# A four-layer graph network on one core: layer 0's input is transposed by DMA in 16-bit halves, and attention's scores and products become separate steps

## Chip, core and metric

The kernel runs on one core of a Trainium2 chip. The metric is device time in microseconds (us) of one execution. The kernel before takes 2674.66 us (median of 3 runs, 2673.68 to 2675.3). The engines are PE (TensorE, matrix products), DVE (VectorE), ACT (ScalarE), POOL (GpSimd) and SP (SyncE, whose queue issues nearly all DMAs here).

## What is computed

The input is x, 64 graphs of 256 nodes with 256 features (f32), and adj, 64 matrices of 256 x 256 (int32). Four layers follow each other; each one is `x = layernorm(x + layer(x, adj))`. Cut to what matters here:

```python
# layer 0: masked attention, 4 heads of 64
q, k, v = x @ Wq.T + bq, x @ Wk.T + bk, x @ Wv.T + bv
attn = softmax(where(adj == 0, NEG, q @ k.T * 64 ** -0.5))
x = layernorm(x + affine_layernorm(attn @ v @ Wo.T + bo))
# layer 1: masked attention on the normed x, 8 heads of 32, then an MLP of width 1024
n = affine_layernorm(x); a = x + softmax(mask(n @ n.T * 32 ** -0.5)) @ n
x = layernorm(x + a + gelu(affine_layernorm(a) @ W1 + b1) @ W2 + b2)
# layer 2: graph attention, one head; layer 3: an edge score by kind of edge, softmax, product
```

The first matmuls of layer 0 contract over the features of x. TensorE contracts over the partitions, so x must be brought with its features on the partitions ("features first"). In memory it lies with the nodes first.

## The kernel before

Two graphs make a group, so there are 32 groups. A group is a Python generator that yields after each step. The program interleaves the groups: in each period it goes through the digits of ORDER, and a digit d runs the next step of the group that started d periods ago. So about six groups are at work at any time. The written order is a wish: a scheduler then places each engine's instructions, only PE's own order is fixed as written.

```python
ORDER = "011225334342343542234235432323132121321132121"
io  = tile_pool(name="io", bufs=2)      # x0 and adj: two buffers each
act = tile_pool(name="act", bufs=3)     # xT, qT, kT, v, y, z, mask ...
ps_s = tile_pool(name="ps_s", bufs=2, space=PSUM)   # scores, two banks each
ps_m = tile_pool(name="ps_m", bufs=4, space=PSUM)   # everything else

def transposed(src, ...):               # PE transposes, then ACT copies out of PSUM
    for c in range(NC):                 # NC = 2 halves of the 256 features
        pt = to_psum(src, c, gs)        # 4 PE transposes of 128 x 128 f32 (L519)
        nc.scalar.copy(dst[:, c, on], pt[:, on])                     # L572
        # or, with scale and bias: nc.scalar.activation(...)         # L574

def attention(qT, kT, v, mask, hd, gamma, behind, tally=None):
    for i in range(G):                  # G = 2 graphs
        for cs in ((0, 1),) if m == 2 else ((0,), (1,)):
            es = scores(i, cs, ...)     # PE scores, ACT exp (L593), DVE mask (L595, L601)
            if before:
                products(*before)       # PE products of the scores of the step before
            go_on()                     # what stands behind a finished graph
            ...
            yield

def layer0(g, x, mask):
    xT = transposed(x)                  # 8 PE transposes a group, 2 ACT copies
    yield
    # WqT, WkT: 8 matmuls of 128 x 512, ACT adds the bias; yield after each; then WvT
    nc.gpsimd.tensor_tensor(x, x, over_blocks(beta0), ALU.add)       # L705
    # attention; behind it: oT * rr (L718), WoT (PE), y (L725), two norms
    # (statistics on DVE, rstd = (var + eps) ** -0.5 on GpSimd, L535 to L539), z (L547)

def layer1(xb, z, mask):
    zT = transposed(z, gamma1, beta1)   # PE transposes of z, ACT L574
    # attention with heads of 32, W1 with Gelu (L774); later W2 (hT), layers 2 and 3

def group(g):
    x, adj = (first, second)[g] if g < 2 else load_group(g)          # L439, L441
    yield
    adjb = io.tile([P, TB, N], BF16, name="adjb", bufs=1)
    nc.scalar.activation(adjb, adj, AF.Copy, accum_out=...)          # L875
    nc.scalar.activation(adj.bitcast(F32), adj, AF.Square, ...)      # L876
    yield
    pt = io.tile([P, G, QB, N], BF16, name="adjT", bufs=1)
    for t in range(TB):                 # 4 DMA transposes, two blocks of 128 x 128 each
        nc.sync.dma_start_transpose(pt[:, i, :, q * P:(q + 1) * P], adjb[:, t, :])   # L883
    yield
    mask = act.tile([P, G, QB * N], BF16, name="mask")
    nc.vector.scalar_tensor_tensor(mask, pt, 1.0, adjb, ALU.mult, ALU.min, ...)      # L886
    xb, z = yield from layer0(g, x, mask)
    ...
```

(Cut and shortened where "..." stands.) At the start the SP queue issues x and adj of group 0, then the weights and constants, then group 1 and the two large weights, and after those the first DMA transposes.

Of the kernel before, what the change touches and what calls it, by code (L numbers as in the profile page):

```python
# [8 lines left out]
F32 = mybir.dt.float32  # L9
BF16 = mybir.dt.bfloat16  # L10
I32 = mybir.dt.int32
U8 = mybir.dt.uint8
AF = mybir.ActivationFunctionType
ALU = mybir.AluOpType
AX = mybir.AxisListType

P = 128
N = 256
D = 256
NC = D // P  # L20
G = 2
QB = N // P
TB = G * QB
T = G * N
# [9 lines left out]
AT_ONCE = 3  # L34


ORDER = "011225334342343542234235432323132121321132121"
PREPARE = 5


# [355 lines left out]
def usual_input(ctx: ExitStack, tc: tile.TileContext, a: dict, out: bass.AP, flag: bass.AP):  # L396
# [7 lines left out]
    nc = tc.nc  # L404
    B = a["x"].shape[0]

    const = ctx.enter_context(tc.tile_pool(name="const", bufs=1))
    io = ctx.enter_context(tc.tile_pool(name="io", bufs=2))
    act = ctx.enter_context(tc.tile_pool(name="act", bufs=AT_ONCE))
# [24 lines left out]
    r_3 = const.tile([P, B // G, TB], F32, name="r_3")  # L434
    last = const.tile([P, B // G, TB], F32, name="last")

    def load_group(g):
        x0 = io.tile([P, TB, D], F32, name="x0")
        nc.sync.dma_start(x0, a["x"][g * G:(g + 1) * G].rearrange("b (q p) d -> p (b q) d", p=P))  # L439
        adj = io.tile([P, TB, N], I32, name="adj")  # L440
        nc.sync.dma_start(adj, a["adj"][g * G:(g + 1) * G].rearrange("b (q p) k -> p (b q) k", p=P))  # L441
        return x0, adj

    def load_rows(name, cols, queue=nc.sync):

# [17 lines left out]
        return t  # L463


    first = load_group(0)
    wqT = load_rows("L0_gnn_WqT", D, nc.scalar)
    wkT = load_rows("L0_gnn_WkT", D, nc.scalar)
    bq = load_column(a["L0_gnn_bq"], D, "bq", nc.scalar)
# [18 lines left out]
    beta2 = load_column(a["L1_gnn_beta2"], D, "beta2")  # L488
    b1 = load_column(a["L1_gnn_b1"], DFF, "b1")
    a0 = load_column(a["L3_gnn_a0"], D, "a0")  # L490
    second = load_group(1)
    w1 = load_rows("L1_gnn_W1", DFF)
    w2 = load_rows("L1_gnn_W2", D)

# [70 lines left out]
    def transposed(src, scale=None, bias=None, gs=ALL):  # L565

        on = tokens(gs)
        dst = act.tile([P, NC, T], F32, name="xT")
        for c in range(NC):
            pt = to_psum(src, c, gs)  # L570
            if scale is None:
                nc.scalar.copy(dst[:, c, on], pt[:, on])  # L572
            else:
                nc.scalar.activation(dst[:, c, on], pt[:, on], AF.Identity, bias=bias[:, c:c + 1], scale=scale[:, c:c + 1])  # L574
        return dst
# [56 lines left out]
    def attention(qT, kT, v, mask, hd, gamma, behind, tally=None):  # L632

        scale = hd ** -0.5
        m = P // hd
        before = sums = None
        after = []

        def go_on():
            for r in list(after):
                if next(r, END) == END:
                    after.remove(r)

        for i in range(G):
            for cs in ((0, 1),) if m == 2 else ((0,), (1,)):
                if cs[0] == 0 and gamma is not None:
                    sums = small.tile([P, QB, NC, 4], F32, name="r1")
                es = scores(i, cs, qT, kT, mask[:, i, :], hd, scale, sums)  # L650
                if before:
                    products(*before)
                go_on()
                if cs[0] == 0:
                    oT = att.tile([P, NC, N], F32, name="oT")
                    zs = att.tile([P, N], F32, name="zs") if sums is None else sums
                if before and before[1][-1] == NC - 1:
                    after.append(behind(before[0], before[5], before[6]))
                before = (i, cs, v, es, hd, oT, zs, gamma, tally)
                yield  # L660
        products(*before)
        after.append(behind(G - 1, oT, zs))
        yield
        while after:
            go_on()
            yield
# [19 lines left out]
            else:  # L686
                nc.vector.tensor_tensor(o, pm, extra[:, i * QB:(i + 1) * QB, 0:D], ALU.add)

    def layer0(g, x, mask):
        xT = transposed(x)  # L690
        yield
        qT = act.tile([P, NC, T], F32, name="qT")
        kT = act.tile([P, NC, T], F32, name="kT")
        for w, bcol, dst in ((wqT, bq, qT), (wkT, bk, kT)):
            for f in range(NC):
                pm = ps_m.tile([P, T], F32, name="pm")
                for c in range(NC):
                    matmul(pm, w[:, c, f * P:(f + 1) * P], xT[:, c, :], start=c == 0, stop=c == NC - 1)
                nc.scalar.activation(dst[:, f, :], pm, AF.Identity, bias=bcol[:, f:f + 1])
            yield  # L700
        v = act.tile([P, TB, D], F32, name="v")
        yield from project(v, xT, wvT, None)
        yield

        nc.gpsimd.tensor_tensor(x, x, over_blocks(beta0), ALU.add)  # L705
        y = act.tile([P, TB, D], F32, name="y")
        z = act.tile([P, TB, D], F32, name="z")
        xb = act.tile([P, TB, D], F32, name="xb", tag="v")

        def behind(i, oT, rz):  # L710

            rr = att.tile([P, NC, N], F32, name="rr")
            lines = dram.tile([NC, 2, N], F32, name="lines")
            nc.sync.dma_start(lines.rearrange("c h n -> (c h) n"), rz[0:P:32, :])
            for h in range(2):
                nc.sync.dma_start(rr[h * 64:h * 64 + 64, :, :], lines[:, h, :].unsqueeze(0).to_broadcast([64, NC, N]))
            yield
            nc.vector.tensor_tensor(oT, oT, rr, ALU.mult)  # L718
            yield
            pm = ps_m.tile([P, QB, D], F32, name="pm")  # L720
            for q in range(QB):
                for c in range(NC):
                    matmul(pm[:, q, :], oT[:, c, q * P:(q + 1) * P], woT[:, c, :],
                           start=c == 0, stop=c == NC - 1)
            nc.vector.tensor_tensor(y[:, i * QB:(i + 1) * QB, :], pm, over_blocks(bop, QB), ALU.add)  # L725
            yield
            mv, rstd = stats(y, i)
            for q, t in enumerate(blocks(i)):
                nc.vector.scalar_tensor_tensor(y[:, t, :], y[:, t, :], mv[:, q, 0:1], gamma0, ALU.subtract, ALU.mult)  # L729
                nc.vector.scalar_tensor_tensor(y[:, t, :], y[:, t, :], rstd[:, 0, q:q + 1], x[:, t, :],  # L730
                                               ALU.mult, ALU.add)
            yield
            mv, rstd = stats(y, i, twice=True)
            scaled(z, y, i, mv, rstd[:, 1])
            for q, t in enumerate(blocks(i)):
                nc.vector.scalar_tensor_tensor(xb[:, t, :], z[:, t, :], rstd[:, 0, q:q + 1], beta1r, ALU.mult, ALU.add)  # L736
            yield

        yield from attention(qT, kT, v, mask, 64, None, behind, [r_0[:, g * G + i:g * G + i + 1] for i in range(G)])
        return xb, z  # L740

# [127 lines left out]
        return (yield from values_of(lambda i, kc, q: e[:, i, at[kc][q]:at[kc][q] + P], x, D, x, r_3[:, g], gs, last[:, g]))  # L869

    def group(g):
        x, adj = (first, second)[g] if g < 2 else load_group(g)
        yield
        adjb = io.tile([P, TB, N], BF16, name="adjb", bufs=1)
        nc.scalar.activation(adjb, adj, AF.Copy, accum_out=there[:, g:g + 1])  # L875
        nc.scalar.activation(adj.bitcast(F32), adj, AF.Square, bias=minus_half, accum_out=edges[:, g:g + 1])  # L876
        yield


        pt = io.tile([P, G, QB, N], BF16, name="adjT", bufs=1)  # L880
        for t in range(TB):
            i, q = divmod(t, QB)
            nc.sync.dma_start_transpose(pt[:, i, :, q * P:(q + 1) * P], adjb[:, t, :])  # L883
        yield
        mask = act.tile([P, G, QB * N], BF16, name="mask")
        nc.vector.scalar_tensor_tensor(mask.rearrange("p g k -> p (g k)"), pt.rearrange("p g k q -> p (g k q)"), 1.0,  # L886
                                       adjb.rearrange("p t k -> p (t k)"), ALU.mult, ALU.min,
                                       accum_out=both_ways[:, g:g + 1])
        xb, z = yield from layer0(g, x, mask)
        y, hT, both = yield from layer1(xb, z, mask)  # L890

        def others(gs):

            yield from project(y, hT, w2, both, b2m, gs)
            x = yield from renormed(y, gs)
            x = yield from layer2(x, mask, gs)
            x = yield from layer3(g, x, mask, gs)
            i, j = g * G + gs[0], g * G + gs[-1] + 1
            nc.sync.dma_start(out[i:j].rearrange("b (q p) d -> p (b q) d", p=P), x[:, gs[0] * QB:(gs[-1] + 1) * QB, 0:D])

        if g < B // G - 1:
            yield from others(ALL)
            return

        parts = [others((i,)) for i in ALL]
        turn = 0
        while parts:
            for r in parts[:turn // QB + 1]:
                if next(r, END) == END:
                    parts.remove(r)  # L910
            turn += 1
            yield
# [62 lines left out]
    for period in range(len(groups) + int(max(ORDER))):  # L975
        for age in ORDER:
            g = period - int(age)
# [61 lines left out]
```

## Time and profile before

| what | value |
|---|---|
| time | 2674.66 us |
| PE busy | 2589.8 us, 97% of the span |
| DVE busy | 1968.5 us, 74% |
| ACT busy | 1291.3 us, 48% |
| GpSimd busy | 587.3 us, 22% |
| DMA queue q1 | 9.9% of 16 engines' span |
| PE transposes of x | 256, 8 in a group |
| ACT copies of the transposed x | 64 of the 130 of L572 |
| DMA transposes of adjb | 128, 4 in a group |

How to read it: a group row of the profile gives the line, the engine, the operation, out<-in by names, then "busy, mean ns of one" and the idle time of the engine just before, with what ended it. Matmul ends are modelled and matmuls overlap, so the sum of their durations says more than they take from PE; where it matters the distance between starts is used. Most f32 matmuls show as two records each, both counted in the "x" of a row; a transpose shows as one. The granted clock is 0.989 of full speed over the span; it is below 1.0 only in the first 150 us or so and at the end, where PE is idle for long.

### The profile page before, as it was taken

The numbers are of one execution on the slowest core, as the hardware profiler recorded it, in microseconds if no ns is written. First come the engines' busy times: TensorE is split into PE (matmuls) and PEld (weight loads), VectorE is DVE, ScalarE is ACT, GpSimd is POOL, SyncE is SP. The second block draws the span as 40 slices with busy tenths as digits, with TensorE's granted clock in tenths as the row PEclk, the third lists the DMA queues.
The fourth block names the chain that finished last, engine by engine and source line by source line (L and its number), as shares of the span: only waits on it lengthen the run. The fifth ranks groups of instructions, "written<-read, shape, count | busy, mean of one in ns | idle before, by whom it ended". The sixth has DMA issues, their size and how long they took to land.

```text
span 2673.3 us, 44868 instructions
## 1 busy us (share of the span) xinstructions
PE 2589.8 (97%) x16648; PEld 1764.3 (66%) x16648; DVE 1968.5 (74%) x6189; ACT 1291.3 (48%) x1995; POOL 587.3 (22%) x1139
## 2 busy tenths in 40 slices
PE   5899999999999999999999999999999999999996
PEld 2466676676676676676676676676676676676665
DVE  4657777777777777777777777777777777777764
ACT  3445444555444555444455444455445455445442
POOL 1212222222222222222222222222222222222221
PEclk8899999999999999999999999999999999999998
DMA  5000110010110010110010110010110010000000
GB/s 154 25 9 22 35 37 25 29 36 21 36 36 25 29 37 21 36 37 25 29 36 21 36 36 25 29 35 22 36 36 25 29 32 25 29 29 17 17 9 17
DMA packets 113728, 83.20 MB, mean 31 GB/s; under 512 B 44256, under 2 KB 113120, under 8 KB 113504
## 3 DMA queue, kind: packets, MB, share of 16 engines
q1 hardware_dynamic: 112416, 79.74, 9.9%
q8 instruction: 134, 2.20, 0.3%
q14 instruction: 90, 0.74, 0.1%
q10 hardware_dynamic: 1088, 0.53, 0.1%
HBM read 54.80 MB, written 17.04 MB: 27 GB/s over the span
## 4 chain that ended last, share of the span: by engine, by line
PE 70%; DVE 17%; POOL 9%; issue 2%; DMA 1%; SPq 1%; ACT 0%; DVEq 0%; POOLq 0%; ACTq 0%
PE pm L516 54%; PE ps L516 10%; PE pm L519 7%; POOL rstd L539 6%; DVE st L532 3%; DVE y L802 2%; DVE y L730 2%; DVE xn L547 2%; POOL ve L535 2%; DVE z L547 2%; DVE mv L533 1%; DVE y L729 1%; DVE xb L736 1%; DVE e L601 1%; DVE r L801 1%
## 5 line engine op out<-in xcount | busy, mean ns | idle before, releaser
L601 DVE SCALAR_TENSOR_TENSOR e<-e,mask 128x256 f32<-128x256 f32 x1024 | 430.3, 486 | 131.6 <-ACT e L593 131.6
L593 ACT ACTIVATE e<-ps 128x1024 f32<-128x1024 f32 x384 | 371.9, 1019 | 195.1 <-PE ps L516 178.4
L516 PE MATMUL pm<-L_gnn_W,hT 128*128 128x256 f32 x2048 | 462.7, 379 | 0.0
L516 PE MATMUL pm<-xT,L_gnn_W 128*128 128x512 f32 x1024 | 456.2, 594 | 0.0
L516 PEld LDWEIGHTS pm<-L_gnn_W,hT 128*128 128x128 f32 x2048 | 384.6, 190 | 48.8 <-issue 0.3
L774 ACT ACTIVATE hT<-pm,b 128x512 f32<-128x512 f32 x256 | 176.9, 691 | 417.7 <-PE pm L516 417.6
L516 PEld LDWEIGHTS pm<-xT,L_gnn_W 128*128 128x128 f32 x1024 | 192.6, 191 | 204.5 <-issue 199.7
L532 DVE BATCH_NORM_STATS2 st<-y 128x6 f32<-128x256 f32 x768 | 301.4, 408 | 6.7
L539 POOL TENSOR_TENSOR rstd<-ve,mhalf 128x2 f32<-128x2 f32 (+1 forms) x384 | 298.1, 776 | 26.6
L547 DVE TENSOR_SCALAR xn<-y,mv,rstd 128x256 f32<-128x256 f32 x384 | 141.6, 410 | 180.1 <-POOL rstd L539 180.1
L535 POOL TENSOR_SCALAR ve<-mv 128x2 f32<-128x2 f32 x384 | 98.5, 257 | 757.7 <-DVE mv L533 757.2
L760 POOL TENSOR_TENSOR both<-y,xb 128x512 f32<-128x512 f32 x64 | 81.3, 1271 | 761.7 <-DVE y L759 761.7
L595 DVE TENSOR_TENSOR e<-e,mask 128x1024 f32<-128x1024 f32 x128 | 150.9, 1221 | 17.1 <-ACT e L593 17.1
L574 ACT ACTIVATE xT<-pm,beta,gamma 128x512 f32<-128x512 f32 x128 | 92.4, 770 | 126.1 <-PE pm L519 125.9
L516 PE MATMUL ps<-xT 32*128 32x256 f32 x2048 | 148.5, 402 | 0.3 <-ACT e L593 0.2
L516 PE MATMUL pm<-e,z 128*32 128x256 f32 x2048 | 141.3, 385 | 1.7 <-DVE e L601 1.4
L516 PEld LDWEIGHTS ps<-xT 32*128 32x128 f32 x2048 | 93.4, 185 | 72.8 <-issue 68.3
L516 PE MATMUL pm<-L_gnn_WoT,oT 128*128 128x256 f32 x512 | 120.4, 389 | 14.7 <-DVE oT L718 12.5
L516 PE MATMUL pm<-e,v 128*32 128x256 f32 x2048 | 125.2, 384 | 6.0 <-DVE e L595 6.0
L516 PE MATMUL ps<-qT,kT 64*128 64x256 f32 x1024 | 127.9, 389 | 0.3 <-ACT e L593 0.3
L516 PE MATMUL pm<-xT,L_gnn_WqT 128*128 128x512 f32 x256 | 121.5, 618 | 3.4 <-ACT xT L572 3.4
L516 PE MATMUL pm<-v,qT 128*128 128x260 f32 x512 | 119.5, 387 | 4.7 <-DVE qT L831 4.7
(136 smaller groups left out, 4058.7 us busy)
## 6 DMA issues: line engine op xcount, KB each, us to landing
x<-in_x SPq DMA_DIRECT2D x32, 512.0 KB
adj<-in_adj SPq DMA_DIRECT2D x32, 512.0 KB
rr<-lines SPq DMA_DIRECT2D x128, 128.0 KB
out<-xn SPq DMA_DIRECT2D x31, 512.0 KB
L_gnn_W<-in_L_gnn_W SPq DMA_DIRECT2D x2, 1024.0 KB
adjT<-adjb SPq DMA_TRANSPOSE x128
lines<-zs SPq DMA_DIRECT2D x64, 4.0 KB
out<-xn SPq DMA_DIRECT2D x2, 256.0 KB
```

Source lines behind the costliest of these rows:

```text
L516: in_order(nc.tensor.matmul(*args, **kw))
L519: in_order(nc.tensor.transpose(*args))
L532: nc.vector.bn_stats(st[:, q, :], src[:, t, 0:D])
L535: nc.gpsimd.tensor_scalar(ve[:, 0], mv[:, :, 1], EPS, None, ALU.add)
L539: nc.gpsimd.tensor_tensor(rstd, ve, mhalf[:, 0:k * QB].rearrange("p (k t) -> p k t", k=k), ALU.pow)
L547: nc.vector.tensor_scalar(dst[:, t, 0:D], src[:, t, 0:D], mv[:, q, 0:1], rstd[:, q:q + 1], ALU.subtract, ALU.mult)
L574: nc.scalar.activation(dst[:, c, on], pt[:, on], AF.Identity, bias=bias[:, c:c + 1], scale=scale[:, c:c + 1])
L593: nc.scalar.activation(e, ps, AF.Exp, scale=scale)
L595: nc.vector.tensor_tensor(e, e, mask.unsqueeze(1).to_broadcast([P, 2, QB * N]), ALU.mult)
L601: nc.vector.scalar_tensor_tensor(e[:, h, k], e[:, h, k], 1.0, mask[:, k], ALU.mult, ALU.mult, accum_out=sums[:, kc, c, j:j + 1])
L760: nc.gpsimd.tensor_tensor(both[:, i * QB:(i + 1) * QB, 0:D], o, xi, ALU.add)
L774: nc.scalar.activation(hT[:, f, :], pm, AF.Gelu, bias=b1[:, f:f + 1])
```

## The change

x is no longer transposed by PE. GpSimd splits each f32 of x into its two 16-bit halves (one copy a graph), the DMA transposes the halves (one transpose a graph, 8 blocks of 128 x 128), and GpSimd joins them to f32 again (two copies a graph). This is meant to take transposes from PE, PSUM buffers from the pool, and copies from ACT. The transposed adj is written straight into the mask tile, which is then multiplied in place. adj has one buffer, the next one being loaded as soon as the two ACT passes have read the present one. Attention yields between scores and the products of the step before, so that other groups' work can stand between them. ORDER is new to suit the new steps. The core of the diff:

```diff
-ORDER = "011225334342343542234235432323132121321132121"
+ORDER = "00012253234343243542234325432123312322122123211312"
@@ loads: x and adj apart
+    def load_adj(g):
+        adj = io.tile([P, TB, N], I32, name="adj", bufs=1)
@@ attention
                 es = scores(i, cs, qT, kT, mask[:, i, :], hd, scale, sums)
                 if before:
+                    yield
                     products(*before)
@@ layer0
-    def layer0(g, x, mask):
-        xT = transposed(x)
-        yield
+    def layer0(g, x, xT, mask):
@@ group
         nc.scalar.activation(adj.bitcast(F32), adj, AF.Square, ...)
+        if g + 1 < B // G:
+            adjs[g + 1] = load_adj(g + 1)
         yield
-        pt = io.tile([P, G, QB, N], BF16, name="adjT", bufs=1)
+        mask = act.tile([P, G, QB * N], BF16, name="mask")
+        mb = mask.rearrange("p g (k q) -> p g k q", k=QB)
         for t in range(TB):
-            nc.sync.dma_start_transpose(pt[:, i, :, q * P:(q + 1) * P], adjb[:, t, :])
+            nc.sync.dma_start_transpose(mb[:, i, :, q * P:(q + 1) * P], adjb[:, t, :])
         yield
-        nc.vector.scalar_tensor_tensor(mask, pt, 1.0, adjb, ALU.mult, ALU.min, ...)
+        nc.vector.scalar_tensor_tensor(mk, mk, 1.0, adjb, ALU.mult, ALU.min, ...)
+        halves = []
+        for i in range(G):
+            xh = io.tile([P, 2, QB, D], U16, name="xh")
+            nc.gpsimd.tensor_copy(xh, x[:, i * QB:(i + 1) * QB, :].bitcast(U16).rearrange("p q (d h) -> p h q d", h=2))
+            xhT = io.tile([P, 2, QB, NC, P], U16, name="xhT")
+            nc.sync.dma_start_transpose(xhT, xh)
+            halves.append(xhT)
+        yield
+        xT = act.tile([P, NC, T], F32, name="xT")
+        for i in range(G):
+            for c in range(NC):
+                nc.gpsimd.tensor_copy(xT[:, c, i * N:(i + 1) * N].bitcast(U16)..., halves[i][:, :, :, c, :])
+        yield
-        xb, z = yield from layer0(g, x, mask)
+        xb, z = yield from layer0(g, x, xT, mask)
```

(The mask and transpose lines are shortened; what is left out is views of the same tiles.)

## The prediction

> **What bounds the kernel now.** I read the page's first part for the busy shares, then the table of busy time by stage, because a mean over the span mixes the filling and emptying of the pipeline with the long middle.
>
> ```profile
> PE 2589.8 (97%) x16648; PEld 1764.3 (66%) x16648; DVE 1968.5 (74%) x6189; ACT 1291.3 (48%) x1995; POOL 587.3 (22%) x1139
> ```
>
> ```profile
> core 0: us, PE busy (x) PEld busy (x) DVE busy (x) ACT busy (x) POOL busy (x), PEclk, DMA share, GB/s
> 0.00:76.00 76.00, 37.31 (x206) 22.28 (x210) 34.03 (x80) 22.91 (x37) 9.93 (x26) 0.82 0.53 142
> ...
> 800.00:1200.00 400.00, 398.28 (x2580) 272.74 (x2583) 304.38 (x956) 200.08 (x309) 91.04 (x174) 1.00 0.10 31
> ...
> 2600.00:2673.00 73.00, 52.91 (x220) 39.26 (x218) 33.32 (x107) 18.02 (x38) 10.45 (x31) 0.91 0.05 16
> ```
>
> In the middle PE idles 1.7 of 400 us; DVE, the next, idles 96. So the middle is PE's queue of instructions, and only what shortens that queue, or makes it wait, counts there. The first 76 us are different: PE idles 39 us, waiting for one group's chain. A period lasts 80.1 us: the transposes of x start at 77.0 us for group 1 and near 2479.8 for group 31, 30 periods apart.
>
> The timeline of PE shows what one group's x transposes take from PE, and what stands around the transposes of z:
>
> ```profile
> 1194.94 1.04 PE L519 MATMUL pm<-ident,x 128*128 128x128 f32 x8
> 1195.81 3.62 PE L516 MATMUL pm<-L_gnn_W,hT 128*128 128x256 f32 x16
> ...
> 1265.94 1.16 PE L519 MATMUL pm<-ident,z 128*128 128x128 f32 x6 [0.28 <-DVE z L547]
> 1266.94 3.62 PE L516 MATMUL pm<-L_gnn_W,hT 128*128 128x256 f32 x16
> 1270.49 1.15 PE L516 MATMUL ps<-xT 32*128 32x256 f32 x16
> ```
>
> The next row begins 0.87 us after the eight transposes began. The group row says 35.0 us busy for 256 of them (1.09 a group), but these durations overlap; 0.87 is the price.
>
> **What the Trainium skill says.** "Perfetto Trace Analysis", section "Identifying the Most-Contended Engine", warns that matmul busy time is a poor measure because pipelined matmuls overlap; the 1.09 against 0.87 us above agrees, so I count distances between starts. "DMA: Bandwidth & Descriptors", section "DMA Transpose (X-bar)", allows the DMA transpose for 2-byte types only, which is why f32 must be split; the trace has it for bf16 alone. "VectorE: DVE Perf Modes", section "The three transpose paths", gives a 128 x 128 bf16 transpose 390 ns on TensorE and 1309 ns by DMA. Here the former costs 109 ns of PE's queue (0.87 / 8, f32), and the latter 1.24 us of issue for two blocks; the gain is that PE, not DMA, is short. "GPSIMD Engine Reference", section "3.1 Elementwise — side-by-side cycle accounting", has one-input work at about 1.03 cycles an element and two-input work near 2.6; at its 1.2 GHz that is 0.86 ns and 2.2 ns. The trace agrees for two inputs (L705: 2421 ns for 1024 elements, 2.36 each) and has no large one-input copy.
>
> **The change part by part.** The removed PE transposes: 0.87 us x 31 groups = 27 us (group 0's lie in the filling). The 64 ACT copies removed (0.59 us each, 38 us) lie on an engine that is half idle: nothing.
>
> The GpSimd copies: a split of 1024 elements is 1024 x 0.86 + 0.18 (what the two-element copy of L786 takes) = 1.06 us, an estimate with that page's rate; a join of 512 is 0.62. A group adds 2 x 1.06 + 4 x 0.62 = 4.6 us; 32 groups 147 us, so GpSimd goes to some 735 us, 27%. Where they stand matters more. In the new instruction order GpSimd does, right after the two long rstd of z, the two splits of a later group, L705 (moved up), and the four joins of the group that comes to WqT next. Its free stretch there is now
>
> ```profile
> 1264.34 1.03 POOL L539 TENSOR_TENSOR rstd<-ve,mhalf 128x4 f32<-128x4 f32 x1
> 1272.38 0.22 POOL L535 TENSOR_SCALAR ve<-mv 128x2 f32<-128x2 f32 x1 [7.01 <-DVE mv L533]
> ```
>
> 7.0 us, and the work is 2.1 + 2.4 + 2.5 = 7.0. It fits, ending at about 1272.4 on this clock. PE wants the joined xT after z's transposes, 8 scores (1.08), 16 W2 matmul records (3.45), the bias row (0.22) and 16 more (3.45): 1266.9 + 8.2 plus the wait below = 1275.7. So 3 us are left, and nothing is lost.
>
> The DMA transposes: the joins belong to a group whose halves were sent a period earlier in the new order, so 80 us cover them. On the SP queue they add, by 1.24 us for two blocks less some 0.45 for an ordinary issue, about 0.4 us a block, 16 x 0.4 + 2 x 0.45 = 7.3 us a period. SP waits for far longer than that (1026.9 us in total for the issue of lines alone, 33 a group). Hidden.
>
> A new neighbour on PE: W2's 16 records no longer stand between the transposes of z and layer 1's first scores. The scores need ACT's first copy of zT:
>
> ```profile
> 1266.70 1.45 ACT L574 ACTIVATE xT<-pm,beta,gamma 128x512 f32<-128x512 f32 x2 [3.20 <-PE pm L519]
> ```
>
> One takes 0.77 us, so it ends at 1267.47, and PE is done at 1266.94: a wait of 0.53 us, x 31 = 16 us lost. Layer 0's scores of both graphs now stand together; with two PSUM buffers and about 1.02 us for each exp, the second graph waits perhaps 0.2 us on average, and its products a little for DVE: 6 us. In return the products have another group's matmuls in front of them, so a late mask costs less. All that can be won back so is what PE waits now: 1.7 us in 400, about 0.35 a period, 11 us.
>
> The filling: group 0's x now goes behind everything on the SP queue.
>
> ```profile
> 11.33 6.74 PE L516 MATMUL pm<-xT,L_gnn_WqT 128*128 128x512 f32 x8 [3.40 <-ACT xT L572]
> ...
> 17.81 6.89 SPq L883 DMA_TRANSPOSE adjT<-adjb x4
> ```
>
> The adj transposes end at 24.7 us, two x transposes of some 4 us or more each follow (under load here 1.7 for two blocks in place of 1.24), landing and joins take 4: the projections begin at about 37 in place of 11.3 us. Some comes back, since the mask (28 us) no longer holds up the products, and PE idles 5.3 us then for a DVE that is busy with setup, and later groups are further along when their turn comes. I take 10 us of loss from a delay of 26; this is a choice.
>
> Sum: -27 + 16 + 6 - 11 + 10 = -6 us, so 2669 us.
>
> **The rivals.** First, **the order pays**: no new wait appears at z, the filling is hidden, the PE saving is kept and more idle is squeezed. For it: ORDER was rewritten, and someone who rewrites it looks at the result. Against it: the middle has only 0.43% of idle to give. It makes 2674.7 - 27 - 11 = 2636 us. Second, **GpSimd becomes a wait**: if a strided 16-bit copy runs at the two-input rate of 2.36 ns, splits cost 2.6 and joins 1.4 us, the joins end at 1265.4 + 5.2 + 2.4 + 5.6 = 1278.6, 3 us behind PE's want, and rstd behind them is late too: +3 us a period, 93 us, 2760 us. For it: no row shows such a copy, and DVE is busy beside it. Against: one input only. Third, **the filling costs its full 26 us** with the waits as summed: 2685 us. Fourth, **the DMA transposes hold the SP queue** so that lines and rr of layer 0 come late: against it 33 us of slack a group; it would show as PE waiting for oT of L718.
>
> **Range and chances.** The certain term is -27; the waits at z and layer 0 are worth +10 to +35, the filling 0 to +26, squeezed idle 0 to -11, and GpSimd 0 to +30 in a mild form. The ends that I find likely are 2630 and 2712. Faster by over 2% needs 2621 us, more than the first rival gives: 0.07. Slower by over 2% needs 2728, a good half of the second: 0.09. The rest, 0.84, is within 2%.
>
> **What would show it.** Rows of transposes of x gone, and PE's count down by 256. In the middle stretch PE idle of about 4 us in 400, led by layer 1's first scores waiting for ACT's zT (right), or under 2 (first rival). The new GpSimd rows near 1.06 and 0.62 us (right) or 2.6 and 1.4 (second rival), and WqT waiting for GpSimd only in the latter. PE's first matmul near 37 us, and 15 us or so more PE idle in the first 76. A period of 79.5 to 80 us. I am wrong if matmul spacing itself changes, if DVE slows down beside GpSimd's copies, or if the emptying at the end, which I left at zero, changes by more than 10 us.

## The result, and the profile after

The changed kernel takes 2914.08 us (median of 4 runs, 2912.69 to 2915.62) against 2674.17 us in the same runs: a ratio of 1.0903, 95% interval 1.0887 to 1.0919. It is 240 us slower, far outside the range.

Line numbers shift by about five: the matmul helper L516 is L521 (L522 in some experiments), transposes L519 are L524 (L525), z's last step L547 is L552 (L554), x + beta0 L705 is L709 (L710), exp L593 is L598 (L600).

The busy shares of the changed kernel, and its busy time by stage (stretch; then busy time and count of PE, PEld, DVE, ACT and POOL; granted clock, DMA share, GB/s):

```profile
PE 2657.2 (91%) x16392; PEld 1779.7 (61%) x16392; DVE 2087.3 (72%) x6189; ACT 1267.2 (44%) x1931; POOL 795.3 (27%) x1331
```

```profile
0.00:76.00 76.00, 30.88 (x177) 18.80 (x178) 25.49 (x47) 19.85 (x33) 14.81 (x25) 0.91 0.52 139
800.00:1200.00 400.00, 376.35 (x2377) 252.72 (x2370) 298.32 (x872) 179.54 (x278) 110.53 (x185) 0.97 0.12 33
```

PE has the 256 transposes less, as it should, and is busy 67 us longer. In the middle it idles 23.7 of 400 us, where it idled 1.7, and its granted clock is 0.97 in place of 1.00. DVE has the same 6189 instructions and is busy 119 us longer: something stretches them. WqT of groups 1 and 31 start at 83.87 and 2486.41 us before, at 95.82 and 2717.92 after: a period was 80.1 us and is 87.4. So some 220 us come from the middle, 12 from the start and the rest from the end.

The waits of the changed kernel (engine, tile, line, waited for: us in total, times, longest):

```profile
DVE mask L894 <- DMA mask<-adjb: 211.8, 32, 9.2
ACT adjb L880 <- DVE mask L894: 210.8, 29, 18.8
PE pm L524 <- DVE z L552: 105.1, 54, 4.4
PE pm L521 <- DVE e L600: 38.1, 31, 1.3
PE pm L521 <- POOL xT L908: 32.6, 1, 32.6
```

PE's largest wait is at the transposes of z, which before was

```profile
PE pm L519 <- DVE z L547: 11.5, 31, 3.1
```

The joins on GpSimd keep PE waiting once, for group 0. DVE's mask multiply waits 6.6 us a group for the DMA transposes, which was 5.3 us in all before.

One z, seen on PE, DVE and GpSimd of the changed kernel (start, length, engine, line, operation):

```profile
1208.61 0.38 PE L524 MATMUL pm<-ident,z 128*128 128x128 f32 x2
1210.88 0.33 PE L524 MATMUL pm<-ident,z 128*128 128x128 f32 x1 [1.89 <-DVE z L552]
1213.30 1.33 PE L524 MATMUL pm<-ident,z 128*128 128x128 f32 x5 [2.09 <-DVE z L552]
1214.65 2.01 PE L521 MATMUL ps<-xT 32*128 32x256 f32 x16
1216.59 3.72 PE L521 MATMUL pm<-L_gnn_W,hT 128*128 128x256 f32 x16
```

```profile
1208.73 0.97 DVE L546 TENSOR_TENSOR rstd<-rstd 128x2 f32<-128x2 f32 x1 [1.70 <-POOL rstd L544]
1209.63 1.19 DVE L552 TENSOR_SCALAR z<-y,mv,rstd 128x256 f32<-128x256 f32 x1
1210.81 2.43 DVE L552 TENSOR_SCALAR z<-y,mv,rstd 128x256 f32<-128x256 f32 x1
```

```profile
1208.66 2.02 POOL L900 COPY xh<-x 128x1024 uint16<-128x1024 uint16 x2
1210.76 2.34 POOL L709 TENSOR_TENSOR x<-x,beta 128x1024 f32<-128x1024 f32 x1
```

Read DVE and GpSimd beside each other. A product of two elements (L546) takes 0.97 us and ends when GpSimd's first split ends; the first half of z takes 1.19 and ends with the second split; the second half takes 2.43 and ends with x + beta0. Undisturbed, the group rows of before have z at 408 ns and L541 at 161 ns. PE stands for 1.89 and 2.09 us with one transpose between, and then runs slowly: 16 score records cover 1.94 us (1214.65 to 1216.59) in place of 1.08, at a granted clock of 0.53 in this stretch, where it was 1.00 before. Three group rows give the sizes (busy, mean ns), the first two of the changed kernel, the third of before:

```profile
L908 POOL COPY xT<-xhT 128x512 uint16<-128x512 uint16 x128 | 121.1, 1008 | 13.6 <-DMA xhT<-xh 13.6
L552 DVE TENSOR_SCALAR z<-y,mv,rstd 128x256 f32<-128x256 f32 x128 | 135.0, 1060 | 0.0
L547 DVE TENSOR_SCALAR z<-y,mv,rstd 128x256 f32<-128x256 f32 x128 | 51.3, 408 | 0.0
```

The Trainium skill has this in "SBUF — State Buffer", section "SBUF: two separate sides": VectorE and GpSimd share one pair of ports under an exclusive lock, held for the whole instruction, taken by a GpSimd operation or by a VectorE operation in a 2-port mode or with two SBUF inputs (the latter only against a GpSimd operation that reads SBUF). The trace agrees in the delay: the delayed operations end within 0.2 us of a GpSimd instruction, however little they have to do themselves. L546 has two SBUF inputs; what makes z one of these operations is not shown by a run here.

The theory after this reading: GpSimd's copies halt DVE just where PE waits for DVE. The rivals: the new order, the mask written in place, the later start.

### The profile page after: what moved, and what is told of

Its sections match the earlier page's. It is cut to its first block, busy times and chain, and to the rows that moved or that the text cites. A ratio compares the mean times of both kernels' runs of the same rounds, so it can differ in the third digit from the quotient of the medians.

```text
span 2910.1 us, 44517 instructions
## 1 busy us (share of the span) xinstructions
PE 2657.2 (91%) x16392; PEld 1779.7 (61%) x16392; DVE 2087.3 (72%) x6189; ACT 1267.2 (44%) x1931; POOL 795.3 (27%) x1331
## 4 chain that ended last, share of the span: by engine, by line
PE 60%; DVE 26%; POOL 10%; issue 2%; DMA 1%; SPq 1%; ACT 1%; ACTq 0%; POOLq 0%; DVEq 0%
PE pm L521 49%; POOL rstd L544 6%; PE ps L521 6%; PE pm L524 5%; DVE z L552 4%; DVE st L537 4%; DVE xn L552 4%; POOL ve L540 3%; DVE y L734 2%; DVE y L806 2%; DVE mv L538 2%; DVE e L600 2%; DVE rstd L546 1%; DVE y L733 1%; DVE xb L740 1%
## 5 line engine op out<-in xcount | busy, mean ns | idle before, releaser
L521 PE MATMUL pm<-L_gnn_W,hT 128*128 128x256 f32 x2048 | 497.3, 398 | 0.0
L606 DVE SCALAR_TENSOR_TENSOR e<-e,mask 128x256 f32<-128x256 f32 x1024 | 364.0, 420 | 160.8 <-ACT e L598 160.8
L540 POOL TENSOR_SCALAR ve<-mv 128x2 f32<-128x2 f32 x384 | 125.1, 326 | 1250.0 <-DVE mv L538 1249.9
L521 PE MATMUL pm<-xT,L_gnn_W 128*128 128x512 f32 x1024 | 460.5, 598 | 0.6
L521 PEld LDWEIGHTS pm<-L_gnn_W,hT 128*128 128x128 f32 x2048 | 404.5, 200 | 89.5 <-issue 29.8
L598 ACT ACTIVATE e<-ps 128x1024 f32<-128x1024 f32 x384 | 372.6, 1022 | 121.0 <-PE ps L521 109.6
L521 PEld LDWEIGHTS pm<-xT,L_gnn_W 128*128 128x128 f32 x1024 | 190.2, 191 | 211.3 <-issue 177.9
L552 DVE TENSOR_SCALAR xn<-y,mv,rstd 128x256 f32<-128x256 f32 x384 | 161.6, 468 | 109.5 <-POOL rstd L544 109.5
L894 DVE SCALAR_TENSOR_TENSOR mask<-mask,adjb 128x1024 bf16<-128x1024 bf16 x32 | 39.2, 1225 | 211.8 <-DMA mask<-adjb 211.8
L524 PE MATMUL pm<-ident,z 128*128 128x128 f32 x256 | 64.1, 372 | 130.5 <-DVE z L552 105.1
L521 PE MATMUL ps<-xT 32*128 32x256 f32 x2048 | 176.0, 462 | 2.4 <-ACT xT L579 1.3
L521 PE MATMUL pm<-e,v 128*32 128x256 f32 x2048 | 130.2, 383 | 38.1 <-DVE e L600 38.1
L600 DVE TENSOR_TENSOR e<-e,mask 128x1024 f32<-128x1024 f32 x128 | 149.8, 1212 | 6.5 <-ACT e L598 6.5
L521 PEld LDWEIGHTS ps<-xT 32*128 32x128 f32 x2048 | 108.0, 215 | 72.4 <-issue 16.1
L521 PE MATMUL pm<-xT,L_gnn_WqT 128*128 128x512 f32 x256 | 117.2, 601 | 32.6 <-POOL xT L908 32.6
L521 PE MATMUL ps<-qT,kT 64*128 64x256 f32 x1024 | 132.3, 398 | 12.6 <-ACT e L598 8.6
L521 PE MATMUL pm<-e,z 128*32 128x256 f32 x2048 | 138.7, 385 | 0.1
```

The costliest lines, as they stand in the source:

```text
L521: in_order(nc.tensor.matmul(*args, **kw))
L524: in_order(nc.tensor.transpose(*args))
L540: nc.gpsimd.tensor_scalar(ve[:, 0], mv[:, :, 1], EPS, None, ALU.add)
L552: nc.vector.tensor_scalar(dst[:, t, 0:D], src[:, t, 0:D], mv[:, q, 0:1], rstd[:, q:q + 1], ALU.subtract, ALU.mult)
L598: nc.scalar.activation(e, ps, AF.Exp, scale=scale)
L600: nc.vector.tensor_tensor(e, e, mask.unsqueeze(1).to_broadcast([P, 2, QB * N]), ALU.mult)
```

## Experiments

Ratios are to the kernel before, in the same runs. Where a diff says only what is replaced, the rest is the kernel named.

### GpSimd beside DVE

**before_splits**: the kernel before, with the two splits added and not used by anything.

```diff
+        for i in range(G):
+            nc.gpsimd.tensor_copy(xs, <halves of x of graph i>)
```

> The kernel before plus the two GpSimd split copies of a group alone (128x1024 uint16, their result is not used, output unchanged); they stand behind the second long rstd of z, as in the changed kernel. Theory 1 (DVE operations with two SBUF inputs[...] stand still while a GpSimd instruction runs): the second graph's z operations stretch from 0.41 us to over 1 us each, PE waits about 2 us more per period for z, plus something for the clock that drops when PE idles: 2730 to 2770 us. Theory 2 (the loss comes from the new order and the mask written in place, GpSimd's copies are harmless): 2670 to 2685 us.

2725.42 us, 1.0179 (1.0162 to 1.0196): slower with no other change, by 50 us, just under the range expected. DVE of this kernel beside its GpSimd:

```profile
1700.03 0.97 DVE L541 TENSOR_TENSOR rstd<-rstd 128x2 f32<-128x2 f32 x1 [1.70 <-POOL rstd L539]
...
1701.25 0.99 DVE L542 TENSOR_TENSOR rstd<-rstd,ve 128x2 f32<-128x2 f32 x1
```

```profile
1699.95 2.27 POOL L887 COPY xs<-x 128x1024 uint16<-128x1024 uint16 x2
```

The halting is shown without anything else of the change: two products of two elements take a microsecond each, and PE waits for the z behind them, 61.1 us in all where it was 11.5:

```profile
PE pm L519 <- DVE z L547: 61.1, 60, 3.9
```

**after_no_beta**: the changed kernel with x + beta0 left out.

```diff
-        nc.gpsimd.tensor_tensor(x, x, over_blocks(beta0), ALU.add)
```

> The changed kernel without GpSimd's x + beta0 (L709, 2.34 us), which is left out (beta0 is all zeros in these inputs). It runs in the middle of the z operations of the second graph. Theory 1: its 2.3 us leave z's delay, 31 times, and some of the slow clock with it: 2800 to 2850 us. Theory 2: 2900 to 2915 us.

2887.88 us, 1.0790 (1.0772 to 1.0808). A miss: only 26 us came back. z's mean falls to 719 ns and no further, since the joins now move up beside it.

**after_act**: the changed kernel with splits and joins on ACT.

```diff
-            nc.gpsimd.tensor_copy(xh, ...)
+            nc.scalar.copy(xh, ...)
-                nc.gpsimd.tensor_copy(xT[...], ...)
+                nc.scalar.copy(xT[...], ...)
```

> The changed kernel with the splits and joins on ACT in place of GpSimd; the DMA transposes and all else stay. Theory 1: z operations back at 0.41 us, the PE saving of 0.87 us a period is there, the new order's waits (0.9 us at layer 1's first scores, about 1.4 us at layer 0's products) and the later start stay: 2680 to 2740 us. Theory 2: 2880 to 2930 us. A third possibility is that ACT's queue becomes a wait for the exps behind the copies: then e waits show in DVE and PE and the time lies between.

2857.61 us, 1.0675 (1.0657 to 1.0692). This missed by far. z is back at 438 ns in the mean, but x + beta0 stayed beside it, and one of z's small products waits for it (DVE, then GpSimd):

```profile
1790.15 2.30 DVE L547 TENSOR_TENSOR rstd<-rstd,ve 128x2 f32<-128x2 f32 x1
```

```profile
1790.01 2.42 POOL L709 TENSOR_TENSOR x<-x,beta 128x1024 f32<-128x1024 f32 x1 [0.29 <-ACT xh L900]
```

Before, x + beta0 waited for the PE transposes of x and so ran later, beside a multiply of e that nobody waited for. With x no longer read by PE, it comes early. But 182 us were still lost, while PE's waits for z come to 65.3 us in all, so there is more than z.

**after_pe_x**: the changed kernel with x transposed by PE, no halves. The new order, the yield and the mask in place stay.

```diff
-        halves = [] ... joins
+        yield
+        xT = transposed(x)
```

> The changed kernel with x transposed by PE again (no halves, no GpSimd copies); the steps, ORDER, the split of scores and products, the mask in place and the one buffer of adj stay. Theory 1: z operations are back at 0.41 us and PE's wait for z below 1 us a period; what is left is the new order's own waits, 0.5 to 1.5 us a period: 2685 to 2725 us. Theory 2: most of the loss stays, 2860 to 2930 us.

2779.79 us, 1.0386 (1.0369 to 1.0404). Missed: 134 us go with the halves, and 104 stay without any. The rivals hold a large part.

### The order, and keeping GpSimd away

**old_order_pool**: the changed kernel without the yield, and with the ORDER of before (one 0 more in front).

```diff
-                    yield
-ORDER = "00012253234343243542234325432123312322122123211312"
+ORDER = "0011225334342343542234235432323132121321132121"
```

> The changed kernel with the order of before: no yield between scores and products, ORDER as before with one more step at the start. The halves, GpSimd's copies and the DMA transposes stay, and so does their place behind the long rstd of z. If the new order alone costs what the changed kernel with PE transposes showed (some 3.8 us a period, at the products of layer 0 and the first scores of layer 1), and the GpSimd copies the rest: 2914 - 31 x 2.8 = 2825, range 2800 to 2850 us. If the order only costs together with the copies it is near 2700; if the copies alone are to blame, near 2900.

2944.22 us, 1.1006 (1.0989 to 1.1023): even slower than the changed kernel, and 94 us above the range expected. Three more kernels keep the old order.

**old_order_pool_pin**: the same, splits and x + beta0 tied behind a later norm on GpSimd.

```diff
+            tc.add_manual_dep(<split, and x + beta0>, <the last rstd on GpSimd>, ...)
```

> As old_order_pool, with the two splits and x + beta0 tied on GpSimd behind a later norm, so that they no longer run while DVE makes z; the four joins still stand behind the long rstd of z (3.9 us). Theory 1 (DVE stands while GpSimd runs): z is only delayed by the first joins, some 2 us; the moved copies now hold up DVE elsewhere, where PE does not wait for it: 2690 to 2760 us, clearly under old_order_pool. If the amount of GpSimd work matters and not its place: as old_order_pool, within 15 us.

2906.29 us, 1.0861 (1.0844 to 1.0877): z at 658 ns, 38 us better than old_order_pool, and 146 above the expected range. The splits moved out of the way, but the joins still run beside z (each half takes 0.92 us for 0.41), and x + beta0 beside an xn.

**old_order_act_late**: old_order_pool with the copies on ACT, and x + beta0 alone tied behind the second norm.

```diff
-            nc.gpsimd.tensor_copy(...)      # splits and joins
+            nc.scalar.copy(...)
+        tc.add_manual_dep(<x + beta0>, <the last rstd on GpSimd>, ...)
```

> Order of before, halves by DMA transposes, splits and joins on ACT, and GpSimd's x + beta0 tied behind the second norm as it stood in the kernel before. Theory 1: nothing on GpSimd stands beside z any more, PE's wait for z is as before, the PE saving of 0.87 us a period shows, and the later start costs 15 to 25 us: 2655 to 2680 us. If DMA transposes or the halves themselves cost something: over 2690 us.

2876.88 us, 1.0757 (1.0741 to 1.0774): 197 us above the range expected. The next kernel shares this miss.

**best**: the same, with group 0 transposed by PE.

```diff
+        if g == 0:
+            yield
+            xT = transposed(x)
+            yield
+        else:
+            <halves>
```

> As old_order_act_late, with group 0 alone transposed by PE as before, so that the start does not wait for the DMA transposes. Expected: 2674 - 27 + a few us = 2645 to 2660 us, faster than the kernel before by 0.5 to 1.1%.

2864.64 us, 1.0708 (1.0693 to 1.0723). Here z is at 407 ns, as before, the start is mended, and 191 us are still missing; the range expected is missed by 205. GpSimd beside z cannot be their cause. What stands out in the waits of this kernel:

```profile
DVE mask L899 <- DMA mask<-adjb: 208.1, 32, 9.5
ACT adjb L885 <- DVE mask L899: 171.0, 29, 7.2
PE ps L522 <- ACT e L600: 92.9, 44, 5.0
```

So the theory grew: the mask in place makes the DMA transposes wait for the last reader of that buffer.

### The mask in place

**before_inplace**: the kernel before, with that part of the change alone.

```diff
-        pt = io.tile([P, G, QB, N], BF16, name="adjT", bufs=1)
+        mask = act.tile([P, G, QB * N], BF16, name="mask")
+        pt = mask.rearrange("p g (k q) -> p g k q", k=QB)
...
-        mask = act.tile([P, G, QB * N], BF16, name="mask")
```

> The kernel of departure with one line of the change alone: the transposed adj goes straight into the mask tile, which is then multiplied in place. In-place theory (the DMA transposes must wait for layer 3's last multiply by the mask that had this buffer before, and the mask, the ACT passes over adj and the exps stand behind them): 2760 to 2820 us, with DVE idle some 6 us a group ahead of the mask multiply for the DMA. Rival (it was late only together with the halves' transposes on the same SP queue): 2670 to 2690.

2808.87 us, 1.0497 (1.0481 to 1.0513): 133 us, from a few lines that change no arithmetic. The chain of one group, on DVE, SP, ACT and PE of this kernel:

```profile
1242.48 1.03 DVE L861 TENSOR_TENSOR qT<-qT,mask 128x512 f32<-128x512 f32 x2
...
1249.94 1.23 DVE L886 SCALAR_TENSOR_TENSOR mask<-mask,adjb 128x1024 bf16<-128x1024 bf16 x1 [6.43 <-DMA mask<-adjb]
```

```profile
1243.54 5.08 SPq L884 DMA_TRANSPOSE mask<-adjb  x4
```

```profile
1251.21 1.06 ACT L875 ACTIVATE adjb<-adj 128x1024 bf16<-128x1024 int32 x1 [8.55 <-DVE mask L886]
...
1253.54 1.91 ACT L593 ACTIVATE e<-ps 128x1024 f32<-128x1024 f32 x2
```

```profile
1254.60 0.70 PE L516 MATMUL ps<-xT 32*128 32x256 f32 x4 [0.35 <-ACT e L593]
```

L861 is layer 3 of the group three before, the last use of the mask in that buffer (there are three). It ends at 1243.51; the transposes start at 1243.54. The mask follows 6.4 us later, then ACT's pass over adj, because adjb has one buffer that the mask must have read, and only then, in ACT's order, the exps that PE waits for. In the kernel before the transposes went into a tile of their own, read only by the mask multiply.

Not all of the 133 us is the transfer's own wait, for the late mask brings on the other cause as well (DVE, then PE):

```profile
1253.92 2.76 DVE L547 TENSOR_SCALAR xn<-y,mv,rstd 128x256 f32<-128x256 f32 x2 [1.14 <-POOL rstd L539]
```

```profile
1257.08 3.12 PE L516 MATMUL pm<-e,z 128*32 128x256 f32 x16 [0.44 <-DVE e L601]
```

An xn, which took 0.73 us before, now runs beside x + beta0 on GpSimd (1253.86 to 1256.20). The multiplies of e stand behind it, and PE's 16 products of e start over 3.05 us in place of 1.00. A group takes 84.49 us in place of 80.08 (from the starts of WqT, 84.46 and 2619.19), so about 2 of the 4.4 us are, as an estimate from these rows, GpSimd beside DVE again. No run here separates the two.

**best_adjT**, **old_order_pool_adjT**, **after_pe_x_adjT**, **after_adjT**: four of the kernels above with the separate tile back. Two KB a partition more have to come from somewhere, so e has seven buffers in place of eight.

```diff
-        mask = act.tile([P, G, QB * N], BF16, name="mask")
+        mb = io.tile([P, G, QB, N], BF16, name="adjT", bufs=1)
...
+        mask = act.tile([P, G, QB * N], BF16, name="mask")
...
-                e = att.tile([P, 2, QB * N], F32, name="e", bufs=8)
+                e = att.tile([P, 2, QB * N], F32, name="e", bufs=7)
```

> The order of the kernel before, copies of the halves on ACT, x + beta0 behind the second norm, group 0 by PE (2864.6 us) with the adj transposes in a tile of their own (e with seven buffers). In-place theory: PE loses its waits for ACT's e and the half clock behind them, and with 27 us of transposes taken from PE it comes to 2645 to 2680 us. Rival (the halves themselves, their DMA transposes on the SP queue and the copies on ACT, are what is late): 2790 us or more, little changed.

2711.85 us, 1.0140 (1.0123 to 1.0157): 153 us back, though not to the range expected.

> The order of the kernel before, halves copied by GpSimd, x + beta0 beside them (2944.2 us), with the adj transposes in a tile of their own. In-place theory: what is left is GpSimd's halting of DVE at z (about 4 us a group) with its clock loss (1 us) and the later start (20 us) less 27: 2790 to 2840 us. If the place of the transposes is nothing: 2930 to 2950.

2833.44 us, 1.0596 (1.0578 to 1.0614): 111 us back, as expected.

> The kernel with the new order and x by PE (2779.8 us, 104 over the kernel of departure), in which now the adj transposes go into a tile of their own instead of the mask's (for the room, one of the eight buffers of e is given up). In-place theory (the DMA transposes must wait for layer 3's last use of that mask buffer, so the mask, the edges and the exps behind it come late): most of the 104 us goes, 2680 to 2705 us, and DVE's idle ahead of the mask multiply that waits for the DMA falls below 1 us a group. Order theory (the yield between scores and products puts e's consumers too near its producers, whatever the mask does): 2760 to 2785 us, with the matmuls of e,v still waiting for DVE's e.

2756.76 us, 1.0308 (1.0291 to 1.0325): only 23 us back, 3 us under the order theory's range; that theory was right here, and 83 us remain.

> The changed kernel (2914.1 us) with only the adj transposes in a tile of their own again (e with seven buffers). GpSimd's halting of DVE at z stays (4.4 us of 7.7 a group by the period table). If the two causes add up: 2800 to 2840 us. If in the new order the mask is not on the path because the z wait hides it: 2890 to 2915.

2913.86 us, 1.0897 (1.0878 to 1.0915): nothing back. In the changed kernel the late mask is not on the path. ACT of the changed kernel shows why:

```profile
1216.70 1.94 ACT L598 ACTIVATE e<-ps 128x1024 f32<-128x1024 f32 x2 [1.25 <-PE ps L521]
1225.44 1.06 ACT L880 ACTIVATE adjb<-adj 128x1024 bf16<-128x1024 int32 x1 [6.80 <-DVE mask L894]
```

The exps of layer 1 stand ahead of adjb there. DVE and ACT wait 210 us each in the table of waits, and it costs nothing.

**before_e7**: a control, the kernel before with seven buffers of e.

> The kernel of departure with seven buffers of e in place of eight, a control for the runs that gave one up for room. If that costs nothing: 2670 to 2680 us. If the eighth buffer matters, some of what is put down to the new order, and of what the repaired versions still lose, is its doing: 2700 or more.

2675.22 us, 1.0000 (0.9991 to 1.0008): the buffer given up costs this kernel nothing.

### What is left: the order, and one instruction on GpSimd

**order_eased**: after_pe_x_adjT with ORDER's end changed, so that a product of layer 1 stands between layer 0's two scores.

```diff
-ORDER = "...22123211312"
+ORDER = "...22123121321"
```

> The new order with x by PE and adj transposed into a tile of its own (2756.8 us, 83 over the kernel of departure), with ORDER changed at one place: in place of layer 0's scores of both graphs back to back, one product of layer 1 (1.0 us) goes between them and the transposes of oT (0.6 us) ahead of the first products of layer 0. Order theory (exp on ACT and the mask multiply on DVE don't get done in the 3 us that PE has between scores and products): the matmuls of e,v lose their wait for DVE and the second scores theirs for ACT, 1.4 + 0.4 us a group, 2695 to 2720 us. Rival (DVE is late for another reason, or the wait moves on to the next consumer): 2740 us or more.

2824.97 us, 1.0553 (1.0537 to 1.0569), 68 us worse where the order theory expected some 50 better; its rival, that the wait moves on, is what came. PE's largest wait of this kernel:

```profile
PE pm L521 <- ACT pm L635: 70.4, 30, 2.4
```

The wait of the second scores for ACT fell from 10.0 to 0.4 us and that for e from 40.3 to 29.1, but a new one came: a PSUM buffer that ACT frees only after DVE's reciprocals of the softmax sums. The wait moved on, so the distance between scores and products is not the whole of what the order costs.

**best_dve**: best_adjT with x + beta0 on DVE, and group 1 by PE too. In best_adjT that addition, though tied behind a norm, still ran beside an xn (DVE, then GpSimd of best_adjT):

```profile
1225.29 2.79 DVE L554 TENSOR_SCALAR xn<-y,mv,rstd 128x256 f32<-128x256 f32 x2 [1.14 <-POOL rstd L545]
```

```profile
1225.23 2.35 POOL L710 TENSOR_TENSOR x<-x,beta 128x1024 f32<-128x1024 f32 x1
```

```diff
-        ins = nc.gpsimd.tensor_tensor(x, x, over_blocks(beta0), ALU.add)   # and its tie
+        nc.vector.tensor_tensor(x, x, over_blocks(beta0), ALU.add)
-        if g == 0:
+        if g < 2:
```

> The order of the kernel before, halves on ACT, adj transposed apart (2711.9 us), with x + beta0 on DVE in place of GpSimd (where it ran beside the second xn, which took 2.8 us for 0.7 and made PE wait 1.7 us a group for e) and groups 0 and 1 transposed by PE. If GpSimd's big instruction beside DVE is the last cause: 2711.9 less 31 x 1.7 less some 10 for the filling, 2645 to 2665 us, faster than the kernel of departure. If a DVE with 1.2 us more to do is late elsewhere: 2690 or more.

2655.59 us, 0.9923 (0.9909 to 0.9936): 20 us faster than the kernel before, the only version that beats it. Of the 56 us to best_adjT, 51 come with the period, and so from GpSimd's addition, and 6 from the start: WqT of groups 1 and 31 start at 95.42 and 2522.69 us there, a period of 80.91, and at 89.44 and 2465.90 here, a period of 79.22. Its middle, by stage:

```profile
800.00:1200.00 400.00, 398.35 (x2595) 270.88 (x2595) 302.38 (x977) 218.85 (x333) 79.20 (x170) 1.00 0.15 37
```

PE idles 1.65 us of 400, as before the change, with eight transposes a group less.

**new_order_repaired**: best_dve with the yield and the ORDER of the changed kernel, and nothing else.

> The repaired version (halves on ACT, x + beta0 on DVE, adj transposed apart, groups 0 and 1 by PE: 2655.6 us) with the yield and the ORDER of the changed kernel; nothing else differs. Order theory (the new order itself costs the 83 us that the version with x by PE kept, and the new neighbour of z, layer 1's first scores, some 0.9 us a group more): 2730 to 2770 us. Rival (the 83 us came from GpSimd's x + beta0, which stood beside layer 3's multiply by the mask there, or from x by PE in an order not made for it): 2655 to 2690.

2839.90 us, 1.0618 (1.0600 to 1.0636), 70 us above the range expected. Order and yield cost 184 us here. Its largest wait of PE, then PE and ACT at z:

```profile
PE ps L521 <- ACT xT L579: 62.2, 31, 2.5
```

```profile
1263.06 1.33 PE L521 MATMUL ps<-xT 32*128 32x256 f32 x16 [2.08 <-ACT xT L579]
1264.32 5.18 PE L521 MATMUL pm<-L_gnn_W,hT 128*128 128x256 f32 x16
```

```profile
1256.77 1.04 ACT L905 COPY xh<-x 128x1024 uint16<-128x1024 uint16 x1 [4.62 <-DMA x<-in_x]
...
1262.23 1.45 ACT L579 ACTIVATE xT<-pm,beta,gamma 128x512 f32<-128x512 f32 x2
```

Layer 1's first scores stand right behind the transposes of z and wait for ACT's zT, which ACT begins only at 1262.23, 2.4 us after PE's last transposes began; PE then runs the next 16 records in 5.02 us (1264.32 to 1269.34, granted clock 0.70) where others take 3.45. ACT is late because it waited 4.62 us for the load of x at the first split, with layer 1's last Gelu, the splits and two exps of layer 3 behind that wait and ahead of zT. best_dve waits as long for this load (158.9 us in all, 157.4 here), but in the old order W2's matmuls cover the copy of zT. So these 184 us are the order's price with the splits on ACT; the changed kernel has none there, and in after_pe_x_adjT, where ACT is free and begins zT 0.76 us after the transposes, and PE's transposes of x stand ahead of the scores, the wait for zT is 0.4 us in all.

## Why the prediction was wrong

| step from the kernel before | us |
|---|---|
| the new order and yield, x still by PE, separate tile (after_pe_x_adjT) | +83 |
| halves by DMA, copied by GpSimd, x + beta0 moved up (after_adjT) | +157 |
| mask in place on top of both (the changed kernel) | 0 |
| sum | +240 |

The parts don't simply add. The halves by GpSimd cost about the same in the old order (2833.44 - 2674.01 = 159), but the mask in place alone costs 133, and the order costs 184 beside halves on ACT. Nor does taking GpSimd's part away return what adding it costs: new_order_repaired, with the copies on ACT, x + beta0 on DVE and two groups by PE, is only 74 us faster than after_adjT: a wait for zT stands where the wait for z was.

- **GpSimd's copies: "It fits ... and nothing is lost". This step failed.** The splits took 1.04 us (1.06 predicted), the joins 1.01 in the mean (0.62 predicted), so that GpSimd was busy 208 us longer and not 147; even so PE waited for a join only in group 0. What failed was treating GpSimd's free 7.0 us as free for DVE. They begin just when DVE makes the second graph's z, the one thing PE wants next. z went from 408 to 1060 ns, PE's wait for it from 11.5 to 105.1 us, and the step of the halves as a whole cost 157 us. The prediction named this case among what would make it wrong, and gave it no term. The trace before had it in sight: at 1276.36 us x + beta0 stood on GpSimd for 2.42 us, and a multiply of e on DVE beside it, begun at 1276.50, took 2.57 in place of 0.42 (its two rows are below). The second rival, GpSimd as a wait, had the engine right and the mechanism wrong: neither the joins nor rstd were late, DVE was.

```profile
1276.36 2.42 POOL L705 TENSOR_TENSOR x<-x,beta 128x1024 f32<-128x1024 f32 x1 [2.97 <-PE pm L519]
```

```profile
1276.50 2.57 DVE L601 SCALAR_TENSOR_TENSOR e<-e,mask 128x256 f32<-128x256 f32 x1
```

- **Layer 0, +6: right in kind, too small.** Its waits, 38.1 us for e on DVE and 8.6 for the exps on ACT, came to 47 us in the changed kernel.
- **The new neighbour, +16: not borne out, its size open.** In the changed kernel PE waits 1.3 us in all for zT, because z itself is late. In new_order_repaired the wait is there and is 2.0 us a group (62.2 / 31) in place of 0.53, but there the splits hold up ACT. What it is with a prompt z and a free ACT is not shown.
- **The clock was left out.** A step of PE's waits has a price behind it: after two stops of 1.89 and 2.09 us the scores took 1.94 us in place of 1.08, at a granted clock of 0.53. The Trainium skill, "TensorE: Matmul & The Clock Gate", section "Part 1: The HAM clock gate", says that the array falls to half its clock after at least one idle window of about 3.4 us. The trace agrees in the size of the slowing. It does not show such a stop without a break: here a transpose stood between the two, and in new_order_repaired a wait of 2.08 us, with sparse transposes ahead of it, brought 0.70 over the next 5.02 us.
- **The mask in place was not examined.** The prediction took it for a saved buffer. In the changed kernel it costs nothing; in the old order it cost 111 to 153 us in three kernels, in before_inplace partly by way of GpSimd beside DVE, and that is more than everything the prediction had in its sum.
- **"Hidden" was right for the halves' own DMA transposes.** Eight blocks took a median of 1.27 us to issue, not some 4, and best_dve is fast with those of 30 groups on its SP queue.
- **The transposes of x, -27, were right.** In best_dve WqT of groups 1 and 31 start at 89.44 and 2465.90 us, a period of 79.22 against 80.08: 0.87 us, the very distance read from the timeline. Group 1 starts 5.6 us later, which leaves the 20 us measured.
- **The filling, +10 from a first matmul near 37 us, was right in size:** it came at 32.6, and group 1 was 12 us late. The 10 was a choice, and so partly luck.

Open is how the order's cost divides: the waits at zT and e are named, and order_eased took some away only to meet another. The single buffer of adj was tested only together with the rest; best_dve has it, so it costs nothing visible in the old order. An order made for the new steps and for a free DVE was not tried.

## What to carry to other kernels

Before giving idle GpSimd time to a new instruction, ask what DVE does in just that stretch and who waits for it: in these traces a DVE operation beside a long GpSimd instruction lasted until that one ended, 2.30 us beside 2.42. Before writing a transfer straight into a tile to save a buffer, find the last reader of the buffer it reuses; here the transfer started 0.03 us after it. And a work item taken from PE pays in full only if every wait that it covered is covered by something else.

## What was not expected of the hardware

- A DVE product of two elements (161 ns in the mean before) took 0.97 us beside a GpSimd copy and 2.30 us beside a two-input GpSimd addition: it ended when that instruction did.
- An 8-block DMA transpose was issued in a median of 1.27 us, a 2-block one in 1.24 us: the issue hardly depends on the blocks here.
- A one-input 16-bit copy of 512 elements on GpSimd took 0.75 us at least and 0.93 in the median in the changed kernel; 1024 elements took 1.04. The prediction's rate held for the splits, not for the joins. How much of the joins' time is DVE's doing is not shown.
